# Five of W2's seven second-level pieces made in the second row's QKV and attention stages instead of in the feed-forward part

## The chip, the cores and the metric

The kernel runs on one core of one Trainium2 chip. The metric is the device time of one execution in microseconds (us); lower is better. The core's engines are TensorE (PE; its weight loads are shown as PEld), VectorE (DVE), ScalarE (ACT), GpSimd (POOL) and SyncE (SP). SP does no arithmetic, it issues DMA transfers; POOL can issue them too, on a queue of its own. Every engine works through its own instructions in order and waits for the others by semaphores.

## The reference

One block of a diffusion transformer with a condition, in fp32, for x of shape 2 x 2048 x 512 (two "rows" of 2048 tokens), 16 heads of 32 and a hidden width of 2048:

```
sh_a, sc_a, gt_a, sh_m, sc_m, gt_m = split(silu(condition) @ Wada + bada, 6)
xm = layernorm(x) * (1 + sc_a) + sh_a
x  = x + gt_a * (causal_attention(xm @ Wqkv) @ Wproj + bproj)
xm = layernorm(x) * (1 + sc_m) + sh_m
h  = gelu(xm @ W1 + b1)
x  = x + gt_m * (h @ W2 + b2)
```

## The kernel before

**The order of the work.** Row 0: QKV, attention, projection; row 1: QKV (it starts among row 0's projection), attention, projection; then the feed-forward part, which treats both rows' tokens in four visits, m = 0 to 3, and in each visit does layer 1 (W1) and then layer 2 (W2). Each engine's order is the order in which the program issues; where side work is put among the main work it is written out by hand, by step numbers.

**The matrix products of the feed-forward part** are done by a two-level scheme of the Strassen-Winograd kind: seven products of smaller blocks take the place of eight, and again seven for eight within each of these. For this the weights are needed in sums. The first-level sums of W1 and W2 (`Quarters`, L1106) are made in row 0's stages and kept in DRAM as `w1d` and `w2d`, each with seven outer pieces named A11, S1, A12, S2, S3, A22, S4. From each outer piece the second level makes a piece of seven blocks: its four quarters, which a load fetches, and four sums of them, which POOL makes one by one in `room_sum` (L1197): S1, S3, S2, S4. The finished pieces lie in DRAM as `w1e` and `w2e`; a piece is 1.75 MB, what is loaded for it 1 MB.

**Where the second-level pieces are made:**

- W1, pieces 0 to 2: in row 1's QKV. `FirstLayer` (L1215) has two rooms `w49`; `also(g, n)` (L1513) is called at each of 48 steps, and at steps 1, 7, 13 a load is issued (`load_blocks`, L1208), three steps later the four sums (128 x 512 each), two steps after those the store, all on POOL and POOL's own DMA queue.
- W1, pieces 3 to 6: in row 1's attention, in eight halves (`FirstHalves`, L1241), by `beside` (L1158), which is also what makes the first-level quarters in row 0's attention. It has one room, `w7`. Each half is: a load on SP's queue (L1255), four sums on POOL (128 x 256 each), a store on SP's queue (L1268), then the next load. `among(now, slack, last)` is called once in every attention step, at its end. It leaves three steps from the end of one half to the next load and three from the load to the sums (the first load is issued at step 0), and it makes one sum in a step, and only where `slack` is true or in the last unit.
- W2, all seven: in the feed-forward part's first visit, m = 0, in layer 2. `Weights.load` (L1601) fetches the four quarters of a piece from `w2d` on SP's queue, `Weights.add` (L1613) makes the four sums on POOL, and behind the fourth it stores the piece to `w2e` on POOL's queue. In the visits m = 1 to 3, and for W1 in all visits, `Weights.load` fetches finished pieces, in two parts of three and four blocks (768 KB and 1 MB), on SP's queue.

**Attention** (`attention_phase`, L563). A row has 16 units: four head groups c of four heads, times four query blocks i of 512 queries. The groups are taken in order; within the first i runs 0, 1, 2, 3, in the others 0, 2, 1, 3. Unit (c, i) has 4i + 3 steps: one for each 128 keys, the last three of them on the diagonal, where the causal mask is needed. In a step PE computes scores st (keys by queries), ScalarE their exponentials e (L619), two tiles of a ring of eight, and two steps later (LAG = 2) PE multiplies them with the values into o. On diagonal steps POOL masks e by affine selects (L628), which o must wait for. On other steps sums of e over several steps, ee, are built (L652 to L664) in place of four separate row sums on PE; they are built by POOL as long as scores of a later unit are still to be made. The tile e is free for a new exponential only after both o and ee have read it. A further line of work on PE (s) and VectorE (mx) prepares the maxima of later units.

**SP's queue in attention.** At the start of unit u `load_queries(u + 3)` issues four transfers `qst` of 256 KB (L348), which PE's s of a later unit needs. At the first unit of a head group (units 0, 4, 8) `load_keys` issues the next group's keys, four transfers `kst` of 1 MB (L339). At the end of a unit `finish` (L673) stores o and the sums. In the last units `prepare` (L438) loads what the projection needs into `kst` and `qst` (`qst<-wide` of 1 MB) and adds to it on POOL (L456). The loads and stores of the half pieces stand among all this, on the same queue.

Of the kernel before, what the change touches and what calls it, by code (L numbers as in the profile page):

```python
# [17 lines left out]
P = 128  # L18
# [9 lines left out]
def dit_block_kernel(  # L28
# [534 lines left out]
    def attention_phase(row, beside=None):  # L563
        b, vv, kst, qst = row.b, row.vv, row.kst, row.qst
        with pool(f"att{b}") as ap, pool(
# [149 lines left out]
            for u, (c, i) in enumerate(units):  # L715
                if NQ <= u + AHEAD < len(units):
                    row.load_queries(u + AHEAD)
                if u % NQ == 0 and c + 1 < C:
                    row.load_keys(c + 1, 0, NG)
                steps = len(steps_of[u])  # L720
                for n_step, tiles in enumerate(steps_of[u]):
                    last = n_step == steps - 1
                    if n_step == 0:
                        summed = set()
                        o = ps_op.tile([P, QB], F32, tag="o", name="o")
                        sm = ps_op.tile([P, QB], F32, tag="sm", name="sm")
# [39 lines left out]

                    def row_sums(es, last, tiles=((0, 0),), sm=sm, summed=summed):
                        first = not summed
                        summed.add(len(summed))
                        tile_by_tile(sm, lambda j, h: ones[:, :HD], es, tiles, first, last)  # L770

                    pending.append((now + LAG, values))
                    sums_of, wait = None, 0
                    if n_step < i * TQ:
                        k = n_step % TQ
                        if k == 0:
                            even = es
# [12 lines left out]
                    if sums_of:  # L790
                        pending.append(
                            (now + LAG + wait, lambda f=row_sums, s=sums_of: f(*s))
                        )
                    if last:
                        pending.append((now + LAG, lambda u=u, o=o, sm=sm: finish(u, o, sm)))
                    pending.sort(key=lambda p: p[0])
                    if among:
                        among(now, n_step >= i * TQ, u + 1 == len(units))
                    now += 1
            flush(now + LAG)  # L800

# [353 lines left out]
                )  # L1155
            )

    def beside(pieces):  # L1158

        def start(pool_):  # L1160

            room = pool_.tile([P, piece], F32, tag="w7", name="w7")
            todo = []

            def among(now, slack, last):
                if not todo and pieces.left():
                    todo.append((now + 3 if now else 0, "load"))
                elif not todo:
                    return
                after, what = todo[0]  # L1170
                if now < after:
                    return
                if what == "load":
                    todo.pop(0)
                    pieces.load(room, nc.sync)
                    todo[:] = [(now + 3, n) for n in range(4)]
                elif what == "store":
                    todo.pop(0)
                    pieces.store(nc.sync)
                elif slack or last:  # L1180
                    todo.pop(0)
                    pieces.make((what,))
                    if what == 3:
                        todo.append((now + 1, "store"))

            return among

        return start

    OUTER = (A11, S1, A12, S2, S3, A22, S4)  # L1190
    OUTER1 = (A11, S1, A12, S2, S3, S4, A22)
    SLOTS = {
        1: {S1: 0, S2: 1, A11: 2, S4: 3, A12: 4, A22: 5, S3: 6},
        2: {S1: 0, S2: 1, A11: 2, A12: 3, S4: 4, A22: 5, S3: 6},
# [17 lines left out]
            room[:, 2:6], src.rearrange("p k (i f) d -> p (k i) (f d)", i=2)  # L1212
        )

    class FirstLayer:  # L1215

        def __init__(self, rooms):
            self.rooms, self.at, self.made, self.stored = rooms, 0, 0, 0

        def load(self):

            act(load_blocks(nc.gpsimd, self.rooms[self.at % 2], 1, self.at))
            self.at += 1

        def make(self):

            room = self.rooms[self.made % 2]
            for k in range(4):
                room_sum(room, 1, k)
            self.made += 1

        def store(self):

            act(nc.gpsimd.dma_start(w1e[self.stored], self.rooms[self.stored % 2]))
            self.stored += 1

    class FirstHalves:  # L1241


        def __init__(self, first):
            self.at, self.loaded, self.made = 2 * first, [], []

        def left(self):
            return self.at < 14

        def load(self, room, queue):  # L1250
            n, half = self.at // 2, self.at % 2
            self.at += 1
            w = room.rearrange("p (n d) -> p n d", n=7)
            src = w1d[:, n].rearrange("p k (i f) d -> p (k i) (f d)", i=2)
            act(queue.dma_start(w[:, 2:6], src[:, :, half * 2 * P : (half + 1) * 2 * P]))  # L1255
            self.loaded.append((n, half, w))

        def make(self, steps):

            for step in steps:  # L1260
                room_sum(self.loaded[0][2], 1, step)
                if step == 3:
                    self.made.append(self.loaded.pop(0))

        def store(self, queue):

            n, half, w = self.made.pop(0)
            act(queue.dma_start(w1e[n][:, :, half * 2 * P : (half + 1) * 2 * P], w))  # L1268

    def project_phase(row, psum, between):  # L1270

# [206 lines left out]
            qkv.run(hp, also)  # L1478
            assert quarters.at == early and not quarters.loaded and not quarters.made

    attention_phase(row, beside(quarters))
    assert quarters.at == FC and not quarters.loaded and not quarters.made


# [1 line left out]
    with pool("qkv1") as qp, pool("ps_qkv1", bufs=6, space=PSUM) as ps_mm:  # L1486
# [20 lines left out]
        with pool("hl1") as hp:  # L1507
            room = [
                hp.tile([P, 7, C * P], F32, tag=f"w49{n}", name="w49") for n in range(2)
            ]  # L1510
            late = FirstLayer(room)

            def also(g, n):  # L1513
                at = g * (C * 2 + MTT) + n
# [4 lines left out]
                if at - 5 in late_loads:  # L1519
                    late.store()  # L1520

            late_loads = range(1, 19, 6)
            qkv.run(hp, also)
            assert late.stored == 3

    halves = FirstHalves(late.stored)
    attention_phase(row, beside(halves))
    assert not halves.left() and not halves.loaded and not halves.made
    ps_s_cm.__exit__(None, None, None)

# [4 lines left out]
    with ExitStack() as mlp:  # L1535
# [58 lines left out]
        class Weights:  # L1594
# [6 lines left out]
            def load(self, at, part):  # L1601
# [628 lines left out]
```

## Time and profile before

| what | us |
|---|---|
| three runs: lowest, median, highest | 2261.32, 2261.87, 2268.04 |
| the profiled execution | 2264.73 |
| its span, first to last instruction | 2263.0 |
| row 0: QKV / attention / projection | 49 to 203 / to 726 / to 786 |
| row 1: QKV / attention / projection | 786 to 961 / to 1486.9 / to 1546.3 |
| feed-forward part, m = 0: layer 1 / layer 2 | 1546.3 to 1632.5 / to 1723.9 |
| feed-forward part, m = 1 / 2 / 3 | to 1901.8 / to 2079.6 / to 2263.0 |

Times within the profile count from the span's start. The granted clock of PE is 0.999 of full speed over the span. A row of groups reads: line of the kernel, engine, operation, out<-in, shapes, count | busy us, mean ns of one | idle time before, and its releaser. A row of the timeline reads: start, duration, engine, line, operation, out<-in, shapes, count in a run, and in brackets the idle time before it with what ended it. A row of windows reads: the stretch, its length, then for PE, PEld, DVE, ACT and POOL the busy time with the number of instructions in brackets, the granted clock, the share of time in which the DMA engines are busy, and GB/s. A row of waits reads: who waited, for whom, us in total, times, the longest.

### The profile page before, as it was taken

To read this page: it belongs to the slowest core of one execution; us is meant where nothing else is said; L and a number is where in the kernel's file an instruction comes from. 1 tells how busy PE (TensorE), PEld (TensorE's weight loads), DVE (VectorE), ACT (ScalarE), POOL (GpSimd) and SP (SyncE) were. 2 spreads that over 40 slices of the span, in tenths; PEclk is the share of its full clock that TensorE was granted. 3 is DMA by queue.
4 is the path that set the end of the run, shared out by engine and by line. 5 is a ranking of instruction groups with operands and counts; after the bars stand their busy time and mean duration, and the time that the engine had idled before them with its cause. 6 is when DMAs were issued, how large, how long until landed. Compare 5 with 4: busy or idle time off the path is not lost. (4 is left out here: it accounts for less than half of the span.)

```text
span 2263.0 us, 34412 instructions
## 1 busy us (share of the span) xinstructions
PE 2237.2 (99%) x12429; PEld 1445.5 (64%) x12429; DVE 1579.7 (70%) x3172; ACT 980.3 (43%) x1909; POOL 1319.5 (58%) x1052
## 2 busy tenths in 40 slices
PE   8999999999999999999999999999999999999999
PEld 3676555555544457655555555447888888888887
DVE  3467777777777525677777777755896876877787
ACT  3334555555565134355555555723432242252231
POOL 4362987989795550078798998563773702602510
PEclk9999999999999999999999999999999999999999
DMA  8769326262244777561622415375476654654643
GB/s 280 246 207 240 63 57 154 55 147 74 64 151 139 260 245 212 168 129 50 147 73 63 109 50 170 122 237 191 142 253 221 211 173 158 205 183 149 221 144 121
DMA packets 144514, 355.66 MB, mean 157 GB/s; under 512 B 14624, under 2 KB 44876, under 8 KB 130648
## 3 DMA queue, kind: packets, MB, share of 16 engines
q1 hardware_dynamic: 137632, 316.72, 47.1%
q0 software_dynamic: 6336, 36.20, 4.4%
q8 instruction: 98, 1.61, 0.3%
q14 instruction: 72, 0.59, 0.1%
q10 hardware_dynamic: 376, 0.55, 0.1%
HBM read 253.80 MB, written 107.48 MB: 160 GB/s over the span
## 5 line engine op out<-in xcount | busy, mean ns | idle before, releaser
L619 ACT ACTIVATE e<-st 128x512 f32<-128x512 f32 (+1 forms) x1152 | 572.3, 578 | 391.4 <-PE st L204 327.6
L484 DVE TENSOR_REDUCE mx<-s 128x1 f32<-128x512 f32 x610 | 412.5, 688 | 190.2 <-PE s L204 187.5
L654 POOL TENSOR_TENSOR ee<-ee,e 128x1024 f32<-128x1024 f32 x204 | 480.4, 2390 | 8.1 <-ACT e L619 8.1
L204 PE MATMUL s<-kst,qst 128*128 128x512 f32 (+3 forms) x1028 | 433.7, 427 | 3.3 <-DVE mx L479 1.0
L204 PE MATMUL st<-qst,kst 128*128 128x512 f32 (+3 forms) x1280 | 380.1, 377 | 0.0
L204 PE MATMUL ps_a<-sum,room 128*128 128x256 f32 x1504 | 356.7, 381 | 3.2 <-DVE c L1698 1.5
L204 PEld LDWEIGHTS ps_a<-sum,room 128*128 128x128 f32 x1504 | 280.8, 190 | 52.1 <-issue 6.0
L204 PE MATMUL o<-e,vv 128*32 128x512 f32 (+3 forms) x2560 | 306.4, 538 | 2.7 <-POOL e L628 2.7
L479 DVE CUSTOM_DVE_ANT_0 junk<-s,causal 128x512 bf16<-128x512 f32 (+3 forms) x418 | 205.4, 491 | 106.8 <-PE s L204 98.9
L204 PEld LDWEIGHTS st<-qst,kst 128*128 128x128 f32 x1280 | 227.5, 188 | 65.3 <-issue 34.5
L204 PEld LDWEIGHTS s<-kst,qst 128*128 128x128 f32 x1028 | 192.9, 188 | 112.9 <-issue 43.7
L654 POOL TENSOR_TENSOR ee<-e 128x1024 f32<-128x1024 f32 x84 | 198.4, 2383 | 98.4 <-ACT e L619 90.8
L628 POOL TENSOR_SCALAR_AFFINE_SELECT e<-e 128x256 f32<-128x256 f32 x256 | 117.1, 492 | 119.0 <-ACT e L619 118.4
L204 PEld LDWEIGHTS <-sel 32*128 32x128 bf16 x1152 | 29.5, 91 | 189.7 <-issue 186.7
L1926 POOL TENSOR_TENSOR c<-c,h 128x512 f32<-128x512 f32 x40 | 58.7, 1487 | 152.9 <-ACT c L1924 152.9
L204 PE MATMUL ps_b<-sum,room 128*128 128x256 f32 x608 | 143.6, 379 | 0.0
L204 PEld LDWEIGHTS o<-e,vv 128*32 128x32 f32 x2560 | 64.2, 108 | 100.6 <-issue 76.6
L204 PEld LDWEIGHTS ps_b<-sum,room 128*128 128x128 f32 x608 | 115.0, 190 | 15.4
L204 PE MATMUL ps_v<-wqkv,xmT 128*128 128x512 f32 x256 | 122.9, 594 | 0.0
L204 PE MATMUL st<-fold,sel 32*128 32x512 bf16 (+1 forms) x1152 | 118.8, 372 | 1.3 <-ACT e L619 0.4
L484 DVE TENSOR_REDUCE mx<-st 128x1 f32<-128x512 f32 x158 | 108.3, 686 | 0.9 <-PE st L204 0.6
L1571 POOL TENSOR_TENSOR sum<-xm 128x256 f32<-128x256 f32 x16 | 15.3, 956 | 153.1 <-PE ps_a L204 153.1
(233 smaller groups left out, 3314.5 us busy)
## 6 DMA issues: line engine op xcount, KB each, us to landing
qst<-q SPq DMA_DIRECT2D x128, 256.0 KB
room<-w1e SPq DMA_DIRECT2D x28, 1024.0 KB
kst<-k SPq DMA_DIRECT2D x24, 1024.0 KB
room<-w1e SPq DMA_DIRECT2D x28, 768.0 KB
room<-w2e SPq DMA_DIRECT2D x21, 1024.0 KB
q<-hl SPq DMA_DIRECT2D x32, 512.0 KB
k<-hl SPq DMA_DIRECT2D x32, 512.0 KB
room<-w2e SPq DMA_DIRECT2D x21, 768.0 KB
```

What stands on the lines that cost most here:

```text
L204: return tc.keep_in_program_order(nc.tensor.matmul(*args, **kw))
L479: nc.vector.tensor_tensor_reduce(junk[:, :w], s[:, :w], causal[:, QB - w :], 1.0, MASKED, ALU.add, ALU.max, m,)
L484: nc.vector.tensor_reduce(m, s[:, :w], axis=AX.X, op=ALU.max)
L619: act(nc.scalar.activation(e[:, h % 2, :w], sts[h][:, :w], AF.Exp))
L628: nc.gpsimd.affine_select(d, d, pattern=[[0, 2], [1, P]], compare_op=ALU.is_ge, fill=0.0, base=0, channel_multiplier=-1,)
L654: act(engine.tensor_tensor(dst, x, y, ALU.add))
L1571: act(engine.tensor_tensor(dst, x, y, ALU.subtract))
L1926: nc.gpsimd.tensor_tensor(c, c, piece_of(base, i, t, pair), ALU.add)
```

## The change

Of W2's pieces only A11 and S1 are still made in the feed-forward part. `FirstLayer` becomes `Late`, which takes a list of (layer, piece), and `FirstHalves` becomes `Halves` in the same way. In row 1's QKV four loads are added at steps 27, 31, 36 and 41, with sums three steps and stores five steps behind them, for A12, S2, S3 and A22 of W2. Row 1's attention makes ten halves instead of eight: the eight of W1 and then two of W2's S4. To fit ten, `beside` gets a number of sums per step (`most`) and a distance in steps (`gap`): 4 and 2 in row 1, 1 and 3 as before in row 0. The caller passes the number of slots of a step: 4 in the last unit; elsewhere 0 off the diagonal, 1 on diagonal steps, and 2 on the steps of units with i = 0. In `Weights.load` the five pieces are fetched finished in m = 0 as well.

The instructions of PE, VectorE and ScalarE and their order are the same in both kernels. POOL has 16 more sums of 128 x 512 in QKV, eight more of 128 x 256 in attention and 20 fewer of 128 x 512 in layer 2 of m = 0; its stores of the five pieces move from there to QKV (four) and to SP in attention (one, as two halves).

```diff
                     if among:
-                        among(now, n_step >= i * TQ, u + 1 == len(units))
+                        among(
+                            now,
+                            4 if u + 1 == len(units) else (n_step >= i * TQ) * (1 + (i == 0)),
+                        )
                     now += 1
...
-    def beside(pieces):
+    def beside(pieces, most, gap):
...
-            def among(now, slack, last):
+            def among(now, slots):
                 if not todo and pieces.left():
-                    todo.append((now + 3 if now else 0, "load"))
+                    todo.append((now + gap - 1 if now else 0, "load"))
                 elif not todo:
                     return
                 after, what = todo[0]
...
                 if what == "load":
                     todo.pop(0)
                     pieces.load(room, nc.sync)
-                    todo[:] = [(now + 3, n) for n in range(4)]
-                elif what == "store":
+                    todo[:] = [(now + gap, n) for n in range(4)]
+                    return
+                if what == "store":
                     todo.pop(0)
                     pieces.store(nc.sync)
-                elif slack or last:
-                    todo.pop(0)
-                    pieces.make((what,))
-                    if what == 3:
-                        todo.append((now + 1, "store"))
+                    return
+                for _ in range(min(slots, most)):
+                    if todo and todo[0][1] in range(4):
+                        what = todo.pop(0)[1]
+                        pieces.make((what,))
+                        if what == 3:
+                            todo.append((now + 1, "store"))
...
+    BEFORE = OUTER[2:]
...
-    attention_phase(row, beside(quarters))
+    attention_phase(row, beside(quarters, 1, 3))
...
-            late_loads = range(1, 19, 6)
+            late_loads = (1, 7, 13, 27, 31, 36, 41)
+            late_pieces = [(1, n) for n in range(3)] + [(2, n) for n in BEFORE[:4]]
+            late = Late(room, late_pieces)
             qkv.run(hp, also)
...
-    halves = FirstHalves(late.stored)
-    attention_phase(row, beside(halves))
+    halves = Halves([(1, n) for n in range(3, 7)] + [(2, n) for n in BEFORE[4:]])
+    attention_phase(row, beside(halves, 4, 2))
...
-                if m or layer == 1:
+                if m or layer == 1 or n in BEFORE:
                     k = slice(0, 3) if part == 0 else slice(3, 7)
                     nc.sync.dma_start(room[:, k], (w1e if layer == 1 else w2e)[n][:, k])
```

More of the change, by code (lines that the diff above doesn't have):

```diff
@@ L1213, in load_blocks, with __init__ @@
         )
-    class FirstLayer:
-        def __init__(self, rooms):
-            self.rooms, self.at, self.made, self.stored = rooms, 0, 0, 0
+    class Late:
+        def __init__(self, rooms, pieces):
+            self.rooms, self.pieces = rooms, pieces
+            self.at, self.made, self.stored = 0, 0, 0
         def load(self):
-            act(load_blocks(nc.gpsimd, self.rooms[self.at % 2], 1, self.at))
+            act(load_blocks(nc.gpsimd, self.rooms[self.at % 2], *self.pieces[self.at]))
             self.at += 1
         def make(self):
-            room = self.rooms[self.made % 2]
+            room, layer = self.rooms[self.made % 2], self.pieces[self.made][0]
             for k in range(4):
-                room_sum(room, 1, k)
+                room_sum(room, layer, k)
             self.made += 1
         def store(self):
-            act(nc.gpsimd.dma_start(w1e[self.stored], self.rooms[self.stored % 2]))
+            layer, n = self.pieces[self.stored]
+            dst = (w1e if layer == 1 else w2e)[n]
+            act(nc.gpsimd.dma_start(dst, self.rooms[self.stored % 2]))
             self.stored += 1
-    class FirstHalves:
-        def __init__(self, first):
-            self.at, self.loaded, self.made = 2 * first, [], []
+    class Halves:
+        def __init__(self, pieces):
+            self.todo = [(*p, half) for p in pieces for half in range(2)]
+            self.loaded, self.made = [], []
         def left(self):
-            return self.at < 14
+            return bool(self.todo)
         def load(self, room, queue):
-            n, half = self.at // 2, self.at % 2
-            self.at += 1
+            layer, n, half = self.todo.pop(0)
             w = room.rearrange("p (n d) -> p n d", n=7)
-            src = w1d[:, n].rearrange("p k (i f) d -> p (k i) (f d)", i=2)
+            src = (w1d if layer == 1 else w2d)[:, n]
+            src = src.rearrange("p k (i f) d -> p (k i) (f d)", i=2)
             act(queue.dma_start(w[:, 2:6], src[:, :, half * 2 * P : (half + 1) * 2 * P]))
-            self.loaded.append((n, half, w))
+            self.loaded.append((layer, n, half, w))
         def make(self, steps):
             for step in steps:
-                room_sum(self.loaded[0][2], 1, step)
+                layer, _, _, w = self.loaded[0]
+                room_sum(w, layer, step)
                 if step == 3:
@@ L1265, in store @@
         def store(self, queue):
-            n, half, w = self.made.pop(0)
-            act(queue.dma_start(w1e[n][:, :, half * 2 * P : (half + 1) * 2 * P], w))
+            layer, n, half, w = self.made.pop(0)
+            dst = (w1e if layer == 1 else w2e)[n]
+            act(queue.dma_start(dst[:, :, half * 2 * P : (half + 1) * 2 * P], w))
     def project_phase(row, psum, between):
@@ L1520, in also @@
                     late.store()
-            late_loads = range(1, 19, 6)
+            late_loads = (1, 7, 13, 27, 31, 36, 41)
+            late_pieces = [(1, n) for n in range(3)] + [(2, n) for n in BEFORE[:4]]
+            late = Late(room, late_pieces)
             qkv.run(hp, also)
-            assert late.stored == 3
-    halves = FirstHalves(late.stored)
-    attention_phase(row, beside(halves))
+            assert late.stored == len(late.pieces)
+    halves = Halves([(1, n) for n in range(3, 7)] + [(2, n) for n in BEFORE[4:]])
+    attention_phase(row, beside(halves, 4, 2))
     assert not halves.left() and not halves.loaded and not halves.made
```

1 line of the change is left out of this document (removed).

## The prediction

> **What bounds the kernel now.** I read the page first: busy time by engine, the chain that ended last, then the costly groups.
>
> ```profile
> PE 2237.2 (99%) x12429; PEld 1445.5 (64%) x12429; DVE 1579.7 (70%) x3172; ACT 980.3 (43%) x1909; POOL 1319.5 (58%) x1052
> PE 30%; DVE 3%; issue 1%; POOL 0%; DVEq 0%
> L204 PE MATMUL o<-e,vv 128*32 128x512 f32 (+3 forms) x2560 | 306.4, 538 | 2.7 <-POOL e L628 2.7
> ```
>
> PE is busy for 2237.2 of 2263.0 us, and the chain names PE far more than anything else. So a change can gain only where PE still waits, and it loses wherever it makes PE wait. Next the windows: the second row's attention, then layer 2 of the feed-forward part for m = 0, 1 and 2, from its first to its last matmul, and the waits of PE in the first of these.
>
> ```profile
> 961.00:1486.00 525.00, 520.50 (x3677) 266.31 (x3677) 384.59 (x912) 302.21 (x606) 431.09 (x310) 1.00 0.39 103
> 1632.53:1723.89 91.36, 89.18 (x425) 77.34 (x424) 81.86 (x87) 27.86 (x49) 57.96 (x39) 1.00 0.70 253
> 1813.64:1901.75 88.11, 88.11 (x425) 77.77 (x424) 68.47 (x87) 27.91 (x49) 8.87 (x7) 1.00 0.51 171
> 1991.47:2079.58 88.11, 88.11 (x426) 77.78 (x425) 68.47 (x87) 27.85 (x49) 8.59 (x7) 1.00 0.52 171
> PE ps_a L204 <- DVE c L1698: 1.5, 2, 0.9
> PE ps_a L204 <- DVE y L1698: 0.7, 1, 0.7
> ```
>
> The 425 matmuls of layer 2 take 91.36 us for m = 0 and 88.11 for m = 1 and 2. That is the only visit in which POOL makes W2's pieces (57.96 us busy against 8.87), and its VectorE needs 81.86 us for the same 87 instructions that cost 68.47 later. PE then waits 2.2 us for VectorE's results. So **all that the making of W2's pieces costs today is 91.36 - 88.11 = 3.25 us**, 0.14% of the span. No placing of them can gain more. In attention POOL is already busy for 431 of 525 us.
>
> **What it removes.** In that visit 20 of 28 sums on POOL and five stores go; the loads of the five pieces grow from 1 MB to 1.75 MB on SP's queue, as m = 1 and 2 already do at 88.11 us. Two pieces stay, A11 and S1, each of four sums. I take the whole 3.25 us; the bounds are 0 (the two that stay slow VectorE just as long) and 3.25. **-3.3 us.**
>
> **QKV of the second row.** Four more pieces: 16 sums, four loads, four stores, all on POOL and its queue.
>
> ```profile
> 49.00:203.00 154.00, 153.87 (x629) 106.58 (x628) 86.68 (x223) 55.92 (x120) 66.99 (x82) 1.00 0.75 234
> 812.00:961.00 149.00, 148.58 (x586) 105.11 (x586) 83.68 (x217) 55.92 (x120) 26.78 (x23) 1.00 0.63 198
> 840.46 5.08 POOL L1206 TENSOR_TENSOR w<-w 128x512 f32<-128x512 f32 x4 [8.43 <-DMA w<-w1d]
> 963.17 0.41 POOL L628 TENSOR_SCALAR_AFFINE_SELECT e<-e 128x256 f32<-128x256 f32 x1 [50.35 <-ACT e L619]
> ```
>
> A piece costs POOL 5.08 us, with up to 8.43 us of standing still for its load, so four cost 20 to 54 us. The first row's QKV ran with POOL at 67 us busy and PE at 153.87 of 154.00; here POOL has 26.78, so 20 us more stay below that. After its last work of this stage POOL idles 50.35 us until attention wants it at 963.17, and the last load is due at step 41 of 48, its sums at 44: at 175/48 = 3.6 us a step from the QKV's start at about 786, near 946, done near 952. I cost it at **0**; were POOL late by a whole load, the first diagonal blocks would wait up to 8 us.
>
> **Attention: a load behind a load.** This is the step that decides. Units 0, 4 and 8 are the first of a head group; each sends the next group's keys, four transfers of 1 MB, on SP's queue. Shown: SP's issues, the DMA traffic of 963 to 981 and of 981 to 984, and POOL.
>
> ```profile
> 960.38 1.96 SPq L339 DMA_DIRECT2D kst<-k  x4
> 962.39 0.47 SPq L1255 DMA_DIRECT2D w<-w1d  x1
> DMA packets 495, 3.67 MB, mean 204 GB/s; under 512 B 48, under 2 KB 48, under 8 KB 48
> DMA packets 584, 0.72 MB, mean 240 GB/s; under 512 B 30, under 2 KB 519, under 8 KB 570
> 969.90 0.41 POOL L628 TENSOR_SCALAR_AFFINE_SELECT e<-e 128x256 f32<-128x256 f32 x1 [0.72 <-ACT e L619]
> 977.79 4.72 POOL L654 TENSOR_TENSOR ee<-e 128x1024 f32<-128x1024 f32 x2 [7.49 <-DMA kst<-k]
> 982.48 9.39 POOL L654 TENSOR_TENSOR ee<-ee,e 128x1024 f32<-128x1024 f32 x4
> 997.22 0.74 POOL L1206 TENSOR_TENSOR w<-w 128x256 f32<-128x256 f32 x1
> ```
>
> The half piece's load is issued at 962.39, right behind the keys. From 963 to 981 the chip moves 3.67 MB, and not one packet between 512 B and 8 KB is among them; the load's rows are 1 KB, and 489 packets of that size pass only from 981 to 984. So the queue serves in the order of issue, the keys take some 20 us at 204 GB/s, and the load lands near 984. Before, nobody minds: the first sum stands at 997.22, as sums are allowed on diagonal steps only after a gap of three. With the gap of two and two slots on the steps of such a unit, POOL's order (the changed kernel's order of instructions) is eight affine selects, **two w sums, then ee**. POOL works in order: it stands from 970.3 to 984, makes two sums of 0.74, and starts ee at 985.5 instead of 977.79: 7.7 us late. Has POOL slack to swallow this? Unit 0's successor says no: from 977.79 on its rows show no idle time. For the next pair of units the rows show it in full, and who waits at its end (the tile e, 1146 to 1153):
>
> ```profile
> 1092.76 1.74 SPq L348 DMA_DIRECT2D qst<-q  x4
> 1094.55 2.87 SPq L339 DMA_DIRECT2D kst<-k  x4
> 1105.04 0.56 SPq L1268 DMA_DIRECT2D w1e<-w  x1
> DMA packets 566, 3.98 MB, mean 210 GB/s; under 512 B 62, under 2 KB 62, under 8 KB 87
> DMA packets 1222, 1.54 MB, mean 309 GB/s; under 512 B 57, under 2 KB 942, under 8 KB 1213
> 1094.53 0.78 POOL L1206 TENSOR_TENSOR w<-w 128x256 f32<-128x256 f32 x1
> 1113.91 4.72 POOL L654 TENSOR_TENSOR ee<-e 128x1024 f32<-128x1024 f32 x2 [7.76 <-ACT e L619]
> 1114.00:1149.00 35.00, 35.00 (x227) 18.07 (x225) 26.95 (x57) 21.08 (x43) 34.92 (x20) 1.00 0.51 129
>   PEld o L204: 0.7, 3
> 1226.78 1.75 SPq L348 DMA_DIRECT2D qst<-q  x4
> 1228.49 0.74 POOL L1206 TENSOR_TENSOR w<-w 128x256 f32<-128x256 f32 x1
> 1247.19 4.73 POOL L654 TENSOR_TENSOR ee<-e 128x1024 f32<-128x1024 f32 x2 [7.21 <-ACT e L619]
> ```
>
> From 1114 to 1149 POOL is busy 34.92 of 35.00 us, and at 1149 PE's o already waits for POOL's e: slack nil. Of the two DMA rows (1099 to 1118, 1119 to 1124) the store issued at 1105.04 again moves only after the keys. In the changed order SP issues at this place: the w1e half store, qst x4, keys x4, the w load. The store waits for the fourth sum, which now takes the place of the one at 1094.53: ready at 1095.3. Nothing on SP passes it, so the queries go late too. Bytes: 0.9 MB of store take 2.8 us (0.9 MB at the 309 GB/s of the row) from 0.9 us after the issue, 1099.0; four query tiles 5.8 (issued at 1092.76, and the keys, which fill 1099 to 1118 and so begin near 1098.5, come right behind), 1104.8; keys 20, 1124.8; the load's 0.5 MB 2 and 0.6 to signal, 1127.4. Two sums: ee starts at 1128.9 and not 1113.91, **15.0 us late**. Unit 8 by the same sum from 1228.49 + 0.74: 1230.2, 1233.0, 1238.8, 1258.8, 1261.4, 1262.9 against 1247.19: **15.7 us**. While POOL stands, ScalarE fills the ring of e tiles (eight, two a step) and stops, and PE with it; then POOL's order, saturated up to the diagonal, hands the rest to o. Unit 12 loads no keys. With a few tenths of slack for each, the three give 7.2 + 14.8 + 15.5 = **37.5 us**. Bounds: half of that, if each pair can run 6 us closer than the busy row shows (18), and 52, if the transfers go at 150 GB/s instead of 204.
>
> **Smaller costs.** The late queries of unit 12 and the last units, where the two halves of S4 put sums in front of affine selects:
>
> ```profile
> 1104.31 0.50 PE L204 MATMUL s<-kst,qst 128*128 128x512 f32 x1
> 1470.32 0.32 SPq L453 DMA_DIRECT2D qst<-wide  x1
> 1473.00 10.96 POOL L628 TENSOR_SCALAR_AFFINE_SELECT e<-e 128x256 f32<-128x256 f32 x8 [6.14 <-ACT e L619]
> 1478.63 1.41 PE L204 MATMUL o<-e,vv 128*32 128x512 f32 x8 [1.63 <-POOL e L628]
> 1448.62 2.61 POOL L1206 TENSOR_TENSOR w<-w 128x256 f32<-128x256 f32 x2 [11.14 <-DMA w<-w1d]
> ```
>
> In unit 4 PE's first product with the new queries stands 11.5 us after their issue (1092.76 to 1104.31). In unit 12, which is alike but for the keys, waiting for the sum 2.5, the store's transfer 2.8 and some 6.5 of start and flow add up to about 1 us more than that: **+1**. At the end PE already waits 1.63 us for POOL. Four sums of 0.74 us ahead of the eight selects, with their load behind the 1 MB of qst issued at 1470.32, put them 1.6 to 3.5 us later: **+2.4**. A unit earlier POOL stands before a w sum as it did at 1448.62, now ahead of six selects: 0 to 5, **+2.4**.
>
> **The sum.** -3.3 + 37.5 + 1 + 2.4 + 2.4 = +40.0 us. The profiled execution took 2264.73 us (span 2263.0 and 1.7 around it): 2304.7. The median of the runs is 2261.87, 2.9 us below it; on that, **2302 us**.
>
> **A rule on the clock.** The kernel shows a granted clock below 1 in one place, after PE's first long wait:
>
> ```profile
> PE ps_c L212 <- DMA wada<-in_L_cond_Wada_dram: 7.6, 1, 7.6
> 20.00:25.00 5.00, 5.00 (x9) 2.04 (x9) 0.38 (x1) 0.68 (x2) 1.05 (x2) 0.73 0.72 261
> ```
>
> After 7.6 us of waiting, 5 us run at 0.73: 1.4 us lost. Units 4 and 8 would each have a standstill of 6 us or more on PE, and two shorter ones. If each of four ended so, 4 x 1.4 = 5.6 us come on top where PE is the later of the two; behind a POOL that is still late they are free. By the Trainium skill, "TensorE: Matmul & The Clock Gate", Part 1, an idle window of about 3.4 us halves the clock until a busy window of that length has passed; the row agrees. The sum keeps this at 0.
>
> **Rivals.** *The load is not held back.* If the small load shares the queue with the keys, it lands after five times its 0.5 MB at 204 GB/s, 12.8 us from 963.3: 976.1, and its two sums end at 977.6, just before POOL's ee at 977.79. Then nothing of the 37.5 remains but some 1.5 us at units 4 and 8: -3.3 + 3 + 1 + 2 = about +3, 2265, not slower by what can be told. It decides at a landing before 976.3. Against it stand the two DMA rows. On that: the Trainium skill, "DMA: Bandwidth & Descriptors", Queues, rings and completion order, says that a later transfer of a queue may finish before an earlier one; the rows show no such overtaking of 4 MB. *Slack that I do not see.* POOL catches up half in each pair: -3.3 + 18 + 3 = +18, 2280. *The clock* falls with each stall: 2302 + 6 = 2308. *Only the gain*: loads are early and the end of attention swallows its sums; 2258.6. *It does not clear the visit*: the two pieces left in the feed-forward part keep VectorE slow; 2305.
>
> **Chances.** Forecast 0.60 (2288 to 2318); clock 0.12 (to 2322); visit not cleared 0.03; half caught up 0.09 (2270 to 2288); load not held back 0.13 (2258 to 2268); only the gain 0.03. 0.3% is 6.8 us, about what a measurement of this kernel can tell from no change. The gain is at most 3.3, so faster by more has 0.01; within it 0.15; slower 0.84. The range 2270 to 2322 holds the first four.
>
> **What would show it.** Right: at the first steps of units 0, 4 and 8 POOL idles before a w sum with the w load as the releaser, about 14, 20 and 20 us; PE waits for POOL's e and for ScalarE's e; attention's 525 us become about 568; layer 2 of m = 0 takes 88 us; QKV is unchanged. Wrong: 1 KB packets among the keys, or w loads landing within 5 us of their issue; POOL with gaps in its ee work of units 1, 5 and 9.

## The result and the profile after

The changed kernel takes 2321.28 us (median of 6 runs, 2314.29 to 2324.62) against 2261.60 us before (6 runs beside it): 1.0257 times as long, 95% interval 1.0236 to 1.0277. That is +59.7 us; the forecast was +40. The profiled execution of the changed kernel took 2324.14 us, its span 2322.4.

Page of the changed kernel; then PE's waits and POOL's waits for loads from 961 to 1546 (who, for whom, us in total, times, longest); then layer 2 of m = 0 from first to last matmul:

```profile
span 2322.4 us, 34422 instructions
PE 2254.5 (97%) x12429; PEld 1451.0 (62%) x12429; DVE 1568.3 (68%) x3172; ACT 980.4 (42%) x1909; POOL 1303.2 (56%) x1059
```

```profile
PE st L204 <- ACT e L619: 19.1, 4, 7.5
PE o L204 <- POOL e L628: 16.1, 8, 5.2
PE s L204 <- DMA qst<-q: 10.5, 3, 4.4
```

```profile
POOL w L1213 <- DMA w<-w1d: 66.6, 4, 21.6
POOL w L1213 <- DMA w<-w2d: 22.9, 2, 15.8
```

```profile
1695.27:1783.38 88.11, 88.11 (x425) 77.78 (x424) 71.05 (x87) 27.86 (x49) 18.12 (x14) 1.00 0.62 212
```

The gain is there in full: the same 425 matmuls take 88.11 us and not 91.36. The loss is all in attention, and it is the one foretold by kind: POOL waits for half-piece loads, 66.6 us for W1's and 22.9 us for S4's, up to 21.6 us at a time, and PE behind it for e. PE now waits 16.1 us for POOL's e, 19.1 for ScalarE's and 10.5 for late queries. Before, in 961 to 1486, it waited for the first two only, and far less:

```profile
PE o L204 <- POOL e L628: 2.4, 3, 1.6
PE st L204 <- ACT e L619: 0.2, 1, 0.2
```

POOL of the changed kernel at the places whose rows of before the prediction shows (units 0, 4, 8), and SP ahead of unit 4:

```profile
970.74 0.41 POOL L628 TENSOR_SCALAR_AFFINE_SELECT e<-e 128x256 f32<-128x256 f32 x1 [0.71 <-ACT e L619]
992.71 1.40 POOL L1213 TENSOR_TENSOR w<-w 128x256 f32<-128x256 f32 x2 [21.56 <-DMA w<-w1d]
994.08 4.65 POOL L654 TENSOR_TENSOR ee<-e 128x1024 f32<-128x1024 f32 x2
...
1110.64 0.73 POOL L1213 TENSOR_TENSOR w<-w 128x256 f32<-128x256 f32 x1
...
1146.30 1.40 POOL L1213 TENSOR_TENSOR w<-w 128x256 f32<-128x256 f32 x2 [20.64 <-DMA w<-w1d]
1147.66 4.64 POOL L654 TENSOR_TENSOR ee<-e 128x1024 f32<-128x1024 f32 x2
...
1261.86 0.75 POOL L1213 TENSOR_TENSOR w<-w 128x256 f32<-128x256 f32 x1
...
1298.16 1.40 POOL L1213 TENSOR_TENSOR w<-w 128x256 f32<-128x256 f32 x2 [19.76 <-DMA w<-w1d]
1299.52 4.65 POOL L654 TENSOR_TENSOR ee<-e 128x1024 f32<-128x1024 f32 x2
```

```profile
1111.40 0.56 SPq L1277 DMA_DIRECT2D w1e<-w  x1
1112.01 3.28 SPq L348 DMA_DIRECT2D qst<-q  x4
1115.33 3.84 SPq L339 DMA_DIRECT2D kst<-k  x4
1119.20 0.68 SPq L1262 DMA_DIRECT2D w<-w1d  x1
```

Two w sums stand right before the first ee of each of these units, and the load that they need was issued last of SP's four. PE's order is the same in both kernels, so each matmul can be paired with itself; by how much it stands later, at the end of each stretch and less what it was late before:

| stretch | forecast | measured |
|---|---|---|
| units 0 and 1 | +7.2 | +15.2 |
| units 4 and 5 | +14.8 | +17.4 |
| units 8 and 9 | +15.5 | +18.9 |
| unit 12 | +1 | +5.1 |
| unit 14 | +2.4 | +1.4 |
| last unit | +2.4 | +3.9 |
| feed-forward part, m = 0 | -3.3 | -3.3 |

With the 0.8 us that PE was late ahead of attention, the measured column makes the 59.4 us by which the span grew.

### The profile page after: what moved, and what is told of

It reads as the page before. It is cut to its first block, busy times and chain, and to the rows that moved or that the text cites. A ratio compares the mean times of both kernels' runs of the same rounds, so it can differ in the third digit from the quotient of the medians.

```text
span 2322.4 us, 34422 instructions
## 1 busy us (share of the span) xinstructions
PE 2254.5 (97%) x12429; PEld 1451.0 (62%) x12429; DVE 1568.3 (68%) x3172; ACT 980.4 (42%) x1909; POOL 1303.2 (56%) x1059
## 4 chain that ended last, share of the span: by engine, by line
PE 44%; DMA 5%; DVE 3%; issue 3%; POOL 3%; SPq 1%; ACT 0%; DVEq 0%; POOLq 0%
PE ps_a L204 15%; PE ps_b L204 7%; PE st L204 6%; PE o L204 4%; PE ps_c L204 4%; PE s L204 3%; DMA w<-w1d 2%; PE ps_o L204 2%; POOL ee L654 2%; DMA qst<-q 1%; PE sm L204 1%; DVE h L1708 1%; DVE sum L1581 1%; PE ps_o L212 1%; PE ps_xt L212 1%
## 5 line engine op out<-in xcount | busy, mean ns | idle before, releaser
L204 PE MATMUL s<-kst,qst 128*128 128x512 f32 (+3 forms) x1028 | 436.0, 429 | 13.7 <-DMA qst<-q 10.5
L204 PE MATMUL o<-e,vv 128*32 128x512 f32 (+3 forms) x2560 | 317.1, 550 | 18.4 <-POOL e L628 18.4
L628 POOL TENSOR_SCALAR_AFFINE_SELECT e<-e 128x256 f32<-128x256 f32 x256 | 111.1, 463 | 102.0 <-ACT e L619 100.7
L1213 POOL TENSOR_TENSOR w<-w 128x256 f32<-128x256 f32 (+1 forms) x68 | 68.5, 1020 | 118.7 <-DMA w<-w1d 75.1
```

Of the source, the lines that this page charges most:

```text
L204: return tc.keep_in_program_order(nc.tensor.matmul(*args, **kw))
L628: nc.gpsimd.affine_select(d, d, pattern=[[0, 2], [1, P]], compare_op=ALU.is_ge, fill=0.0, base=0, channel_multiplier=-1,)
L1213: act(nc.gpsimd.tensor_tensor(room[:, slot[d]], room[:, slot[x]], room[:, slot[y]], op))
```

## The experiments

The theory to be tested: the close pacing puts two sums ahead of POOL's ee in units 0, 4 and 8, their load stands behind 4 MB of keys, and PE cannot pass POOL. Rivals: the added sums themselves are too much for POOL; the pieces in QKV delay attention; the traffic of all queues together.

**Only the QKV part.** Four W2 pieces in QKV; eight halves and the old pacing in attention; S4 stays in the feed-forward part.

```diff
-    BEFORE = OUTER[2:]
+    BEFORE = OUTER[2:6]
...
-    halves = Halves([(1, n) for n in range(3, 7)] + [(2, n) for n in BEFORE[4:]])
-    attention_phase(row, beside(halves, 4, 2))
+    halves = Halves([(1, n) for n in range(3, 7)])
+    attention_phase(row, beside(halves, 1, 3))
```

> Only the QKV part of the change: four pieces of W2 (A12, S2, S3, A22) are made in the second row's QKV, attention keeps the pacing and the eight halves of before, and A11, S1 and S4 stay in the feed-forward part. Theory (the half pieces' loads behind the keys stop POOL in attention, the pieces in QKV cost nothing by themselves): no wait of POOL for a load in units 0, 4 and 8, layer 2 of m = 0 at 88 to 90 us, so 2258.5 to 2262. Rival (the work in QKV, with its last store among the row's own transfers, delays attention): PE waits at attention's start, 2265 to 2275.

2261.22 us (12 runs) against 2263.98 before on the same chip: 0.9988 (0.9980 to 0.9996). The theory's forecast held (2258.5 to 2262): the QKV part alone gains 2.8 us, and the interval only just leaves out no change. Layer 2 of m = 0 in this kernel:

```profile
1632.27:1720.75 88.48, 88.37 (x425) 77.69 (x424) 73.45 (x87) 27.86 (x49) 24.24 (x19) 1.00 0.61 215
```

2.9 of the 3.25 us are saved with S4 still made there. Of all the versions here this is the only one whose interval lies below the kernel of before.

**Only the pacing.** No W2 piece is moved; the eight halves of W1 get gap 2 and the new slots.

```diff
-    BEFORE = OUTER[2:]
+    BEFORE = ()
...
-            late_loads = (1, 7, 13, 27, 31, 36, 41)
+            late_loads = (1, 7, 13)
-            late_pieces = [(1, n) for n in range(3)] + [(2, n) for n in BEFORE[:4]]
+            late_pieces = [(1, n) for n in range(3)]
...
-    halves = Halves([(1, n) for n in range(3, 7)] + [(2, n) for n in BEFORE[4:]])
+    halves = Halves([(1, n) for n in range(3, 7)])
```

> Only the pacing: attention's eight halves of W1 with a gap of two, two slots on the steps of units with i = 0 and up to four in the last, all seven W2 pieces in the feed-forward part as before. Theory (the pacing alone puts the sums of units 0, 4 and 8 behind the keys): the loss of the change less what its unit 0 loses to the later keys (about 8 us) and less the 4 us of the last unit, but without the 3.2 us gained in the feed-forward part, about 2261.6 + 16 - 8 + 17 + 19 + 5 + 1 = 2312 (2302 to 2318). Rival (it is the added work, 8 more sums in attention and 16 in QKV): 2262 to 2268.

2316.75 us, 1.0236 (1.0220 to 1.0252). 52.8 us of loss without one piece moved: it is the pacing, far more than the added work. What the pieces add, by pairing the matmuls, is 5 us in unit 0 and 5 in the last unit, less the 3.3 gained. Gap and slots were changed together here; which of the two matters is not separated. POOL's wait in unit 0 is shorter than in the changed kernel (21.56 us):

```profile
986.90 1.43 POOL L1213 TENSOR_TENSOR w<-w 128x256 f32<-128x256 f32 x2 [16.54 <-DMA w<-w1d]
```

**The half pieces' loads on ScalarE's queue.**

```diff
-    def beside(pieces, most, gap):
+    def beside(pieces, most, gap, queue=nc.sync):
...
-                    pieces.load(room, nc.sync)
+                    pieces.load(room, queue)
...
-    attention_phase(row, beside(halves, 4, 2))
+    attention_phase(row, beside(halves, 4, 2, nc.scalar))
```

> The change with one difference: the loads of the half pieces in the second row's attention are issued by ScalarE, on its own queue, and not by SP; stores stay on SP. Theory (the load waits its turn on SP's queue behind 4 MB of keys): each load lands within 3 to 8 us of its issue though the keys are moving, POOL's waits of 20 us before the w sums of units 0, 4 and 8 shrink below 6 us, and with them PE's waits for ScalarE's and POOL's e there; what stays are the late queries of units 4, 8 and 12 (about 16 us with the clock) and the end of attention (5): 2272 to 2290. Rival (the sums themselves, two a step, are what POOL has no time for): as the change, 2310 to 2325. Rival (all queues share the traffic so that the load is as late as before): as the change.

2328.61 us, 1.0287 (1.0274 to 1.0301): no better than the change. Here my theory's forecast failed and the third rival's held. The load went out at 962.49, the keys were moving, and the sums still had to wait. The row of POOL names the query transfers as releaser, but the load's own last packet ends at 986.61, 1.0 us ahead of the sums. Shown: POOL; the traffic of 968 to 984 by queue (q1 is SP's, q10 ScalarE's); ScalarE's wait for the store that must land before a new load:

```profile
987.62 1.41 POOL L1213 TENSOR_TENSOR w<-w 128x256 f32<-128x256 f32 x2 [18.03 <-DMA qst<-q]
```

```profile
q1 hardware_dynamic: 444, 3.09, 86.6%
q10 hardware_dynamic: 445, 0.46, 14.4%
```

```profile
ACT e L619 <- DMA w1e<-w: 23.1, 4, 10.8
```

444 packets of the one queue and 445 of the other passed in these 16 us: one for one. But the keys' packets are 8 KB and the load's 1 KB, so half a megabyte still takes as long as four: the load's last packet ends 24.1 us after its issue, and POOL waits 18.03 us and not 21.56. The Trainium skill, "DMA: Bandwidth & Descriptors", Queues, rings and completion order, has the engines go round the queues packet by packet; these counts agree. A queue of its own is thus no way past the keys for a transfer in small packets, and ScalarE, waiting for the stores, lost 23.1 us besides. That the load must wait its turn *in one queue* was too narrow: it lands with the keys in either.

**QKV's W2 loads earlier.**

```diff
-            late_loads = (1, 7, 13, 27, 31, 36, 41)
+            late_loads = (1, 7, 13, 19, 25, 30, 35)
```

> The change with the four W2 loads of QKV at steps 19, 25, 30, 35 and not 27, 31, 36, 41, so that the last store (1.75 MB) is through before the row's last q and k go out. Theory (the last store of QKV, from 944 to 950 us of the profile, pushes back SP's queue and so the keys at attention's start by some 5 us, and the first half piece's load with them): POOL's first wait for the load falls from 21.6 to about 14 to 17 us, the rest as in the change: 2310 to 2318. Rival (the keys start later for another reason): as the change, 2314 to 2325, with the first wait still above 20 us.

2320.98 us, 1.0258 (1.0240 to 1.0275). The first wait fell as forecast, from 21.56 to 16.58 us:

```profile
990.15 1.44 POOL L1213 TENSOR_TENSOR w<-w 128x256 f32<-128x256 f32 x2 [16.58 <-DMA w<-w1d]
```

That equals the 16.54 of the run without any W2 piece in QKV: QKV's last store costs the keys, and with them the load, 5.0 us (the edit moves all four pieces; that it is the last store alone is argued). The total did not fall, and the forecast of 2310 to 2318 was missed: PE lost 3.9 us within QKV, between 870 and 912 us, where the earlier pieces now move. The run with five pieces in QKV, below, shows the first of these places too.

**The load ahead of the keys.** One difference: in units 0, 4 and 8 of row 1 the keys are issued after the first step.

```diff
-                if u % NQ == 0 and c + 1 < C:
+                if u % NQ == 0 and c + 1 < C and b == 0:
                     row.load_keys(c + 1, 0, NG)
...
+                    if b and n_step == 0 and u % NQ == 0 and c + 1 < C:
+                        row.load_keys(c + 1, 0, NG)
                     now += 1
```

> The change with one difference: in the second row's units 0, 4 and 8 the four key transfers are issued after the unit's first step, behind the half piece's load instead of ahead of it; queue, sums, slots and bytes are those of the change. Theory (the load waits while 4 MB of keys pass): POOL waits under 6 us for the loads of these units, PE's waits there for ScalarE's and POOL's e go, and what stays are the queries held up by the store (some 16 us with the clock) and the end of attention (5): 2261.6 - 3.2 + 16 + 5 = 2279 (2268 to 2288). Rival (two sums a step, or ten halves, are too much for POOL wherever the load lands): 2310 to 2325.

2286.66 us, 1.0099 (1.0078 to 1.0119): 34.6 us less than the change, with the same sums, slots and bytes. POOL's and PE's waits in attention:

```profile
POOL w L1215 <- DMA w<-w1d: 5.6, 4, 4.3
```

```profile
PE s L204 <- DMA qst<-q: 10.1, 3, 3.8
PE o L204 <- POOL e L628: 5.3, 1, 5.3
```

POOL's 66.6 us of waits for these loads are down to 5.6, and PE's for ScalarE's e are gone but for 0.2. The first rival falls, and so does the third as a reason for the whole loss, since the bytes are the same and only their order differs. What is left is what the theory left: late queries and the end. By pairing, the late queries cost 6.1, 6.2 and 5.0 us in units 4, 8 and 12 here. In the changed kernel the first two were hidden behind POOL, so that taking away POOL's waits does not win back all that units 0, 4 and 8 had lost.

**The same, with the half pieces' stores on POOL's queue.**

```diff
-    def beside(pieces, most, gap):
+    def beside(pieces, most, gap, queue=nc.sync):
...
-                    pieces.store(nc.sync)
+                    pieces.store(queue)
...
-    attention_phase(row, beside(halves, 4, 2))
+    attention_phase(row, beside(halves, 4, 2, nc.gpsimd))
```

> As the run with the load first, and the half pieces' stores in the second row's attention go on POOL's own queue, so that SP does not stand before the next queries until the fourth sum is made. Theory (the store ahead of the queries makes them late): PE's 10 us of waits for qst in units 4, 8 and 12 go, with the clock they cost; the gain of the feed-forward part and the end of attention (0 to 6) remain: 2258 to 2268. Rival (the queries are late from the store's transfer itself or the traffic): as the run with the load first, 2275 to 2288.

2273.18 us, 1.0040 (1.0027 to 1.0054): another 13.5 us less. PE's waits for qst are gone; two of more than 1 us remain, both in the last unit:

```profile
PE o L204 <- POOL e L628: 5.3, 1, 5.3
PE sm L204 <- DVE ee L654: 4.7, 1, 4.7
```

So the store ahead of the queries did make them late. The end of attention costs more here than in the changed kernel (by pairing, the last unit makes PE 10.4 us later, there 3.9), so the forecast of at most 2268 was missed.

**The same without S4 in attention.** As the last run, with `BEFORE = OUTER[2:6]` and eight halves.

> As the run with the load first and the stores on POOL's queue, but attention makes only the eight halves of W1; S4 stays in the feed-forward part with A11 and S1. Theory (what is left of that run's loss, about 12 us at the end of attention, comes from S4's two halves in the last unit; two sums a step and a gap of two cost nothing in themselves): the last unit ends as before, layer 2 of m = 0 at 88.5 us, 2259 to 2264. Rival (the close pacing itself, or the stores on POOL's queue, cost time at the end): 2268 to 2275.

2264.08 us, 1.000 (0.999 to 1.001). The end of attention's loss goes with S4's halves. Two sums a step and a gap of two cost little in themselves once the load is ahead of the keys and the store is out of the queries' way: by pairing, PE comes 1.0 us later at two places of attention and makes most of it good at the end, 0.6 us in all. The 2.9 us that layer 2 of m = 0 is shorter do not show in the median: the two together would give 0.9990, the lower end of the interval.

**All five pieces in QKV.** Eight loads there, the old pacing and eight halves in attention.

```diff
-            late_loads = (1, 7, 13, 27, 31, 36, 41)
-            late_pieces = [(1, n) for n in range(3)] + [(2, n) for n in BEFORE[:4]]
+            late_loads = (1, 7, 13, 19, 25, 30, 35, 40)
+            late_pieces = [(1, n) for n in range(3)] + [(2, n) for n in BEFORE]
...
-    halves = Halves([(1, n) for n in range(3, 7)] + [(2, n) for n in BEFORE[4:]])
-    attention_phase(row, beside(halves, 4, 2))
+    halves = Halves([(1, n) for n in range(3, 7)])
+    attention_phase(row, beside(halves, 1, 3))
```

> All five pieces (S4 too) made in the second row's QKV, eight loads at steps 1, 7, 13, 19, 25, 30, 35 and 40; attention with eight halves and the pacing of before. Theory (nothing in attention is touched, the feed-forward part keeps only A11 and S1): layer 2 of m = 0 at 88.1 us, 2258.5 to 2261. Rival (an eighth piece in QKV makes POOL or its queue late at attention's start): 2264 to 2275.

2264.97 us, 0.9995 (0.9985 to 1.0004), above the 2258.5 to 2261 of the forecast. Layer 2 of m = 0 gains its 3.3 us, but within QKV PE comes 4.4 us later, and it stands once for something that the profile does not name:

```profile
872.54 0.30 PE L204 MATMUL s<-kst,qst 128*128 128x128 f32 x1 [2.59 <-issue]
```

The run with early W2 loads loses time at the same matmul, the changed kernel and the run with the QKV part alone, whose W2 loads begin later, do not. In the next run, which adds transfers there and no sums, the same matmul waits too, and there the profile names the keys:

```profile
875.06 0.30 PE L204 MATMUL s<-kst,qst 128*128 128x128 f32 x1 [2.33 <-DMA kst<-k]
```

That the added traffic is the cause here as well is argued from this, not shown.

**The clock by itself.** Two runs on the kernel of before. In the first, extra transfers were to hold up three weight loads of the feed-forward part.

```diff
+        LATE = {
+            17: [(0, 7, 0), (0, 2, 1)],
+            31: [(0, 7, 0), (0, 5, 1)],
+            45: [(0, 7, 0), (0, 7, 1)],
+        }
...
+                if part == 0 and at in LATE:
+                    for lo, hi, src_n in LATE[at]:
+                        nc.sync.dma_start(spare_d[:, lo:hi], w1e[src_n][:, lo:hi])
```

> The kernel of before with three transfers added on SP's queue in the feed-forward part, each ahead of one load of a weight piece (third piece plus one of layer 1 for m = 1, 2 and 3): 2.25, 3.0 and 3.5 MB from DRAM to DRAM, so that PE waits for that piece for some 2 to 20 us, once in a visit, with nothing else changed. Theory (a long standstill of PE lowers its clock for some microseconds after it): after a wait of over 3.4 us the granted clock is 0.5 for 3 us or more, and the visit grows by the wait plus 1.5 us or more; after a shorter one it stays near 1. Rival (the clock falls for another reason, such as the load on the other engines in attention): each visit grows by its wait alone, with the clock at 1.

2271.24 us, 1.0024 (1.0013 to 1.0034), and no answer: nothing held the transfers back to their place, and SP issued them between 828.6 and 893.6 us, in QKV, where PE came out 4.4 us later. In the second a weight load is repeated into the same room, which keeps it in its place:

```diff
+        AGAIN = {17: 3, 31: 4, 45: 6}
...
+                    for _ in range(1 + (AGAIN.get(at, 0) if part else 0)):
+                        nc.sync.dma_start(
+                            room[:, k], (w1e if layer == 1 else w2e)[n][:, k]
+                        )
```

> The kernel of before; in the feed-forward part the second part (1 MB) of one weight piece in each of m = 1, 2 and 3 is loaded 4, 5 and 7 times into the same room, one behind the other, so that PE waits once in each visit, for some 5, 10 and 20 us, with nothing else changed. (This mends the former run on the clock, whose extra transfers went out in the second row's QKV and kept PE from nothing in the feed-forward part.) Theory (a long standstill of PE lowers its clock after it): beside each wait of over 3.4 us the granted clock is 0.5 for some 3 us or more after PE works again, and the visit grows by the wait plus 1.5 us or more. Rival (the clock falls for another reason, in attention only): each visit grows by its wait alone, clock at 1.

2311.2 us (one run). PE waited three times, 6.33, 14.18 and 24.34 us. The windows just behind each wait:

```profile
1771.00:1774.00 3.00, 2.15 (x5) 1.82 (x6) 0.07 (x1) 0.00 (x0) 0.00 (x0) 0.50 1.04 421
1774.00:1776.00 2.00, 2.00 (x8) 1.63 (x8) 1.15 (x2) 0.00 (x0) 1.27 (x1) 0.72 0.89 355
1965.00:1970.00 5.00, 4.77 (x12) 3.88 (x13) 1.37 (x2) 0.00 (x0) 1.48 (x2) 0.53 0.70 266
1970.00:1973.00 3.00, 3.00 (x16) 2.64 (x15) 2.10 (x4) 0.00 (x0) 3.00 (x4) 1.00 0.03 9
2169.00:2174.00 5.00, 4.28 (x10) 3.50 (x11) 1.18 (x2) 0.00 (x0) 1.26 (x1) 0.50 0.06 21
```

Beyond the wait itself PE lost 1.4, 2.3 and 2.3 us (by pairing the matmuls), here in the feed-forward part, so that the rival which ties the clock to attention falls. In this run the price of a standstill is its length and some 2 us, whether it lasts 14 us or 24.

## Why the prediction was right, and where its sum was short

**Right by its steps.** The gain (-3.3, measured -3.3). The place and kind of the loss: POOL stands before two w sums in units 0, 4 and 8 for loads behind the keys, by the pacing alone (only the pacing: 2316.75; load ahead of the keys: -34.6 us). The step "slack nil": by the rows above the first ee is late by 994.08 - 977.79 - 0.8 = 15.5, 1147.66 - 1113.91 - 16.1 = 17.7 and 1299.52 - 1247.19 - 33.4 = 18.9 us (what PE was late already is taken off), and PE comes out of these stretches 15.2, 17.4 and 18.9 us later. PE took over POOL's lateness to within half a microsecond. The late queries and the last unit were named too, and the runs that take them away gain 13.5 and 9.1 us.

**Too small by a third in all.** The forecast was +40, the change cost +59.7. The time of 2321.28 lies above the 2288 to 2318 that the prediction kept for its own sum, and inside its range by 0.7 us only because that reached on to 2322 for a falling clock. What the sum lacked came mostly from elsewhere (next), so that the range still held was luck.

**Too small: the load's arrival.** The term "7.2 + 14.8 + 15.5 = 37.5 us" measured 51.5.

- The term "keys 20", with "the load's 0.5 MB 2 and 0.6 to signal" behind it, is some 3 us short everywhere. From the sum that frees the store to the next w sum I had 32.1 us in unit 4 (1095.3 to 1127.4) and 32.2 in unit 8; the rows give 1146.30 - 1111.37 = 34.9 and 1298.16 - 1262.61 = 35.5. Unit 0's 16.54 us of waiting without the W2 pieces, against 984 - 970.3 = 13.7, is 2.8 more too. Most of it is the keys: by the packets of the trace they take 23.0 us in unit 4 and 23.5 in unit 8 from the start of the first to the end of the last. The load's last packet ends 2.2 and 2.1 us after that, and the sums start another 1.0 and 1.3 us later; the 0.6 is shown by no row. A mean rate tells when most of a transfer has passed, but the sum waits for its last packet. At 1140.9, where the forecast, 16.1 us later, has the keys end in unit 4, 14 of their 512 packets and 495 of the load's 512 are still to come (the traffic of 1140.9 to 1145.4):

```profile
DMA packets 781, 1.09 MB, mean 243 GB/s; under 512 B 48, under 2 KB 543, under 8 KB 766
```

- "I cost it at 0" for QKV was right for the time of QKV and wrong for what follows: its last store, issued on POOL's queue at 942.29, delays the keys by 5.0 us (21.56 against 16.54 and 16.58). I had asked only whether POOL would be late, and had not counted the store's bytes against the transfers of SP's queue. Before the change nothing would have minded, as the run with the QKV part alone shows; it is the close pacing that makes it count. 2.8 and 5.0 make up the 7.8 by which unit 0's ee was later than the forecast 7.7.

**Too small: unit 12.** The "about 1 us more" measured 5.1. The terms, 2.5, 2.8 and 6.5, add up to 11.8, which is only 0.3 above the 11.5, and the clock was kept at 0. Here no POOL is late, and the late queries and the clock show bare. PE's first product with them, and the windows behind it:

```profile
1425.96 0.77 PE L204 MATMUL s<-kst,qst 128*128 128x512 f32 x1 [2.69 <-DMA qst<-q]
```

```profile
1426.00:1432.00 6.00, 6.00 (x25) 2.05 (x26) 1.38 (x2) 0.66 (x2) 1.78 (x3) 0.50 1.04 377
1432.00:1434.00 2.00, 2.00 (x10) 1.31 (x9) 1.26 (x4) 1.36 (x3) 0.00 (x0) 0.99 1.04 388
```

A wait of 2.69 us and 6 us at half clock, which put PE another 2.4 us behind.

**The clock, as a rival.** It fell as that rival says, and more often than four times: nine stretches of attention show it at 0.5, for 3.4 to 10.2 us each, and PE's busy time for the same instructions grew by 2254.5 - 2237.2 = 17.3 us. But it is only a small part of why the sum was short. In units 0, 4 and 8 PE's lateness is POOL's, so there the slower matmuls only filled time in which PE would have waited for POOL anyway, as the prediction held ("behind a POOL that is still late they are free"). It shows where nothing else is late, in unit 12. Adding all 17.3 us to the 40 would come near the total by accident.

**Wrong: a rival's reason.** "If the small load shares the queue with the keys, it lands after five times its 0.5 MB": with a queue of its own it did share, packet by packet, and landed with the keys' last packets. The share goes by packets and not by bytes.

## What to carry to other kernels

Before a sum is moved closer behind its load, look at what stands ahead of the load, in bytes and in packets, and at who stands behind the sum on its engine: a gap of some steps may be hiding a queue. Where an engine runs without idle time up to the point at which another waits for it, a stall of it passes on one for one (here 15.5 us as 15.2), so price it by the landing of the load, and count with it every store shortly before, also one on another queue. A gain of 3 us in one stage is best taken with moves that leave the tightly paced stages alone, as the QKV part by itself does.

## What the runs showed of the hardware that was not expected

- **The clock falls after short waits too.** Behind a wait of 1.75 us (for POOL's e, at 1176.07 us of the changed kernel) the granted clock was 0.5 for some 3 us; behind waits of 1.02 us there, and 1.63 us before the change, it stayed at 1:

```profile
1176.00:1177.00 1.00, 0.93 (x6) 0.38 (x8) 0.00 (x0) 0.00 (x0) 1.00 (x3) 0.51 0.00 0
1177.00:1178.00 1.00, 1.00 (x8) 0.00 (x0) 0.00 (x0) 0.00 (x0) 1.00 (x1) 0.50 0.00 0
```

  The Trainium skill, "TensorE: Matmul & The Clock Gate", Part 1, gives an idle window of about 3.4 us as what it takes; here half of that was enough. All nine low stretches in attention last 3.41 us or two or three times that; why the 1.63 us before the change did not start one is not shown.
- The share between two queues by packets, in the run with the loads on ScalarE's queue, was the other surprise.
- **One VectorE sum at times takes 5.8 us and not 0.9.** In five of the twelve profiled executions, seven times in all, a `sum<-xm` of the feed-forward part takes that long; PE then waits 2.4 us for VectorE and comes out 2.4 to 3.7 us later. The profiles of the kernel before and of the changed kernel have none, that of the run with the load ahead of the keys has two. The sum before the change, and the second of these two with PE's wait behind it:

```profile
1778.81 0.94 DVE L1571 TENSOR_TENSOR sum<-xm 128x256 f32<-128x256 f32 x1
1804.23 5.85 DVE L1583 TENSOR_TENSOR sum<-xm 128x256 f32<-128x256 f32 x1
1811.28 3.54 PE L204 MATMUL ps_a<-sum,room 128*128 128x256 f32 x8 [2.37 <-DVE c L1710]
```

  What sets it off is not shown. A difference of 2 to 4 us between two single executions is thus not yet one between two kernels.
